# Preparing the next image in a fused two-layer kernel: vector steps three sample products apart, the norm's reciprocal in four pieces

## The chip, the cores and the metric

The kernel runs on one core of a Trainium2 chip. The metric is the device time of one execution in microseconds. Engines are named as in the profile: PE is TensorE's matmul and PEld its weight load, DVE is VectorE, ACT is ScalarE, POOL is GpSimd, SP is SyncE, which only issues DMAs here. A "q" after an engine's name is its sequencer.

## The reference

Two layers over x of shape (32, 128, 32, 32), each added to its input. Both begin with a group norm over 32 groups.

```python
# layer 0: a state-space block over the 1024 positions of an image
h = einsum('bdl,de->ble', u, W_enc) + b_enc        # 128 -> 1024
y = gelu(causal_conv(h, K of 64 taps) + D * h)
g = y @ W_glu + b_glu                              # 1024 -> 2048
g = g[..., :1024] * sigmoid(g[..., 1024:])
h = layernorm(h + g)
x = x + (h @ W_dec + b_dec)                        # 1024 -> 128

# layer 1: a deformable depthwise convolution, 8 x 8 taps
off = depthwise_conv_3x3(gn(x), offset_w) + offset_b   # 2 x 64 offsets a position
for each of 64 taps: acc += weight[c, tap] * bilinear(gn(x), position + tap + off)
x = x + gelu((acc - bn_mean) * bn_gamma / sqrt(bn_var + 1e-5) + bn_beta)
```

All of it is in float32.

## The kernel before

Three short stages build the convolution's kernel table, normalise the input and run layer 0's encoder and convolution; they end at about 2100 us and are not touched. The rest is `main_block`, which runs two generators side by side.

`first_part(b)` is the gate, norm and decoder of layer 0 for image b, in two halves of 512 positions. For each of eight groups m it runs eight matmuls for the gate (L707), eight for the value (L730) and one for the encoder (L746); the decoder (L639) follows one group late. ACT applies the sigmoid (L714), DVE multiplies (L738) and adds (L759), ACT squares (L767), and POOL sums (L641, L768). At the end of a half, `close` forms mean and variance with two matmuls and leaves the rest to five small closures. Each is put on a list by `later(n, work)`: after every matmul of the gate `tick()` counts down, and a closure runs when its count is out.

`second_part(b)` is layer 1 for image b as matmuls: 68 pieces, each with three sample products, which makes 204 steps. A piece needs two loads from DRAM, `ds` and `dhy` (hat functions of the sampling coordinates, 512 KB each at full width, L978 on SP's queue). DVE multiplies them (`weights`, L989) two pieces ahead of their use. Each step is one matmul (L1032) into one of four PSUM buffers, and a DVE multiply by the tap weights out of it (L1035); POOL adds up (L1044, L1049). There are five buffers for `ds` and four for `dhy`, and a load waits until its buffer is free. Pieces 32 to 35 have half the width, so steps 96 to 107 are short. Image windows `dxw` (L1003) are loaded on SP's queue as well.

`prepare(b + 1)` makes what `second_part(b + 1)` needs, in small closures put between the steps of `second_part(b)`. A list of pairs (step, closure) says before which of the 204 steps each is issued. In the order of the list before: `fetch` loads the image that layer 0 stored (L793, SP); `total`, `mean`, `variance` and `normal` are the group norm (ACT at L798, L805 and L813, tiny matmuls, DVE at L816 and L817); nine `taps` are the 3 x 3 offset convolution (DVE, L835 and L839); `largest` keeps the maximum (L847); `across` and `down` turn offsets into coordinates (L856, L867); `spread(0)` and `spread(1)` store them to DRAM with eight DMAs each (L874, SP); `turn(0)` and `turn(1)` transpose the image on PE (L922), copy it by ACT (L923) and store it (L926, ACT's queue); `gather(0)` and `gather(1)` load the coordinates spread out (L888, SP); 24 `hats` make the hat functions, two ACT instructions each (L903, L904) and a store of 312 KB (L905, ACT's queue); `ready` hands the image over.

Within an engine and within a queue, instructions keep the order in which the program issues them. `run_along` lets the generator that is behind in its own costs go next: a tick costs 863, a step its columns plus 40. An image takes 290 ticks and 204 steps. The tiles of the fetched image, the offsets, the coordinates, the transposed image and two tiles of the image's end share two buffers (tag `img`).

The last two images have no `first_part` beside them.

Of the kernel before, what the change touches and what calls it, by code (L numbers as in the profile page):

```python
# [14 lines left out]
P = 128  # L15
# [485 lines left out]
def main_block(nc, tc, const, ins, x, u_d, y_d, x1_d, out, offmax):  # L501
# [20 lines left out]
    with ctx:  # L522
# [78 lines left out]
        for i in range(2):  # L601
            t = dram1.tile([2, NCOL], F32, tag=f"rel_d{i}", name=f"rel_d{i}")
            flat = t.rearrange("a (p l) -> (a p) l", p=P // 2)
            n = 2 * NCOL // P
# [5 lines left out]
        def at(t, offset, ap):  # L610
            return bass.AP(tensor=t.tensor, offset=t.offset + offset, ap=ap)
# [22 lines left out]
        def temp(name):  # L634
            return tpool.tile([P, T], F32, tag="gt", name=name)
# [9 lines left out]
        def later(calls, work):  # L645

            soon.append([calls, work])
# [8 lines left out]
        def close(b, hf, sums, dec, xt):  # L656

            tag = f"{b}_{hf}"
            m1, d, rs = (temp(f"g{n}_{tag}") for n in ("m1", "d", "rs"))
            ps = pglu.tile([P, T], F32, tag="g", name=f"gpm_{tag}")  # L660
            nc.tensor.matmul(ps, const["davg"], sums[0], start=True, stop=True)
            nc.scalar.copy(m1, ps)
            ps = pglu.tile([P, T], F32, tag="g", name=f"gpq_{tag}")
            nc.tensor.matmul(ps, const["davg"], sums[1], start=True, stop=True)
            nc.scalar.activation(rs, m1, AF.Square)

            def variance():
                nc.vector.scalar_tensor_tensor(
                    d, m1, neg_g, dec, op0=ALU.mult, op1=ALU.add
                )  # L670
                nc.vector.tensor_sub(rs, ps, rs)

            def deviation():
                nc.scalar.activation(rs, rs, AF.Sqrt, bias=const["eps"])

            def scale():
                nc.vector.reciprocal(rs, rs)
                nc.vector.tensor_mul(d, d, rs)

            def add():  # L680
                nc.vector.scalar_tensor_tensor(xt, d, shift, xt, op0=ALU.add, op1=ALU.add)

            def store():
                nc.scalar.dma_start(x1_d[b, :, hf * T : hf * T + T], xt)
                stored.add((b, hf))

            later(2, variance)
            later(4, deviation)
            later(7, scale)
            later(8, add)  # L690
            later(11, store)

        stored = set()
        pending = {}
# [1 line left out]
        def first_part(b, last=False):  # L696
            for hf in range(2):
# [5 lines left out]
                for m in range(KD):  # L703
# [37 lines left out]
                    if "close" in pending:  # L741
                        close(*pending.pop("close"))
                        yield 2 * MM
                        tick()
# [26 lines left out]
            if last:  # L771
                decode(pending.pop("decode"))
                close(*pending.pop("close"))
                while soon:
                    yield MM
                    tick()
# [6 lines left out]
        def prepare(b):  # L783
# [37 lines left out]
            def taps(lo, hi):  # L821
                def run():
                    if lo == 0:
                        st["co"] = two.tile([P, L], F32, tag="img", name=f"dco_{b}")
                    co3 = st["co"].rearrange("p (h w) -> p h w", w=W)
                    v3 = st["v"].rearrange("p (h w) -> p h w", w=W)
                    for n in (4, 0, 1, 2, 3, 5, 6, 7, 8)[lo:hi]:
                        dy, dx = n // 3 - 1, n % 3 - 1
                        y0, y1 = max(0, -dy), H - max(0, dy)
                        x0, x1 = max(0, -dx), W - max(0, dx)  # L830
                        src = v3[:, y0 + dy : y1 + dy, x0 + dx : x1 + dx]
                        to = co3[:, y0:y1, x0:x1]
                        wn = off_w[:, n : n + 1]
                        if n == 4:
                            nc.vector.tensor_scalar(  # L835
                                to, src, wn, off_b, op0=ALU.mult, op1=ALU.add
                            )
                        else:
                            nc.vector.scalar_tensor_tensor(  # L839
                                to, src, wn, to, op0=ALU.mult, op1=ALU.add  # L840
                            )

                return run
# [25 lines left out]
            def spread(a):  # L869
                def run():  # L870
                    for ky in range(8):

                        g = a * 8 + ky
                        nc.sync.dma_start(  # L874
                            at(
                                rel_d[b % 2],
                                a * NCOL + ky // KY2 * NPIECE + 7 * SLOT + ky % KY2 * H,
                                [[7 * SLOT, 8], [8 * SLOT, W], [1, H]],
                            ),
                            st["rel"][g * 8 : (g + 1) * 8],  # L880
                        )

                return run

            def gather(a):
                def run():
                    t = st["t", a] = one.tile([P, HSUB], F32, tag=f"rel{a}", name=f"dr_{b}_{a}")
                    nc.sync.dma_start(  # L888
                        t, at(rel_d[b % 2], a * NCOL, [[HSUB, P], [1, HSUB]])
                    )  # L890

                return run

            def hat(a, k):


                def run():
                    if k == 0:
                        st[f"h{a}"] = dram.tile(
                            [(8, 16)[a], NCOL], F32, tag=f"hat_d{a}", name=f"dhat_{b}_{a}"  # L900
                        )
                    t = hatpool.tile([P, HSUB], F32, tag="hat", name=f"dh_{b}_{a}_{k}")
                    nc.scalar.activation(t, st["t", a], AF.Abs, bias=minus[:, k : k + 1])  # L903
                    nc.scalar.activation(t, t, AF.Relu, scale=-1.0, bias=const["one"])  # L904
                    nc.scalar.dma_start(  # L905
                        at(st[f"h{a}"], k * NCOL, [[HSUB, P], [1, HSUB]]), t
                    )

                return run

            hats = [hat(0, k) for k in range(8)] + [hat(1, k) for k in range(16)]

            def turn(n):


                def run():
                    if n == 0:
                        st["vt"] = two.tile([P, NCHUNK, C], F32, tag="img", name=f"dvt_{b}")
                    ps = psam.tile([P, 4, C], F32, tag="sam", name=f"dtr_{b}_{n}")
                    for i in range(4):  # L920
                        lo = (4 * n + i) * P
                        nc.tensor.transpose(ps[:, i, :], st["v"][:, lo : lo + P], ident)  # L922
                    nc.scalar.copy(st["vt"][:, 4 * n : 4 * n + 4, :], ps)  # L923
                    if n == 1:
                        st["vt_d"] = dram.tile([L, C], F32, tag="vt_d", name=f"dvt_d_{b}")
                        nc.scalar.dma_start(  # L926
                            st["vt_d"].rearrange("(n p) c -> p n c", p=P), st["vt"]
                        )

                return run  # L930

            def ready():
                images[b] = st["vt_d"], [st["h0"], st["h1"]]

            steps = [
                (34, fetch), (41, total), (43, mean), (46, variance), (48, normal),
                *((49 + i, taps(i, i + 1)) for i in range(9)),
                (58, largest), (59, across), (60, down), (61, spread(0)), (62, spread(1)),
                (64, turn(0)), (66, turn(1)),
                (68, gather(0)), (69, gather(1)),  # L940
                *((75 + 102 * i // len(hats), step) for i, step in enumerate(hats)),
                (178, ready),
            ]
            return steps
# [128 lines left out]
        def opening():  # L1073

            yield 30.0
            for _, step in prepare(0):
                step()
                yield 1.0
            for i in range(SB):
                load_hat(i, 0)  # L1080
            for i in range(HB):
                load_hat(i, 1)
            windows(0, 0)
            weights(0)
            weights(1)
# [5 lines left out]
        for b in range(B):  # L1091
            steps = prepare(b + 1) if b + 1 < B else []
            if b + 2 < B:
                run_along(
                    (first_part(b + 2, last=(b + 2 == B - 1)), FIRST),
                    (second_part(b, steps), SECOND),
                )
            else:
                run_along((second_part(b, steps), SECOND))
# [152 lines left out]
```

## Time and profile before

| | us |
|---|---|
| median of 9 runs | 14057.63 |
| range of the runs | 14050.15 to 14072.49 |
| the profiled execution | 14059.32 |
| its span, first to last instruction | 14057.3 |
| first sample step | 2329.6 |
| one image in the regular part | about 370 |
| image 30, without layer 0 beside it | 328 |

The profile is of one execution. Its page gives busy times and the chain of waits; further views give the waits by pair, the busy time in chosen windows and the instructions in order of time. A row of a timeline has start, length, engine, line, operation, result and operands, and in brackets the idle time before it and what ended it. Images are counted from 0; image 10 starts at 6023.0 us and image 11 at 6392.4. Step numbers of an image are found by counting the weight loads of L1032, two to a step.

### The profile page before, as it was taken

Reading aid. Unit: us, or ns where it says so; the run is one execution under the profiler, and the core shown is the slowest. Engines: PE = TensorE matmul, PEld = TensorE weight load, DVE = VectorE, ACT = ScalarE, POOL = GpSimd, SP = SyncE. Lnnn points to the kernel's source line nnn. Section 1 sums busy time; section 2 is a strip of 40 time slices with the busy share of each in tenths; the row PEclk is TensorE's granted clock in tenths of the full one; section 3 lists DMA queues with packets and bytes.
Section 4 is the critical chain, followed back from the end, with each engine's and each line's share of the span. In section 5 each row is a group of like instructions: output and inputs, shape, how many; then the busy total and the mean of one; then the engine's idle time right before and its main releaser. Section 6 shows DMA issues by size and latency. Waiting matters only on the chain.

```text
span 14057.3 us, 134776 instructions
## 1 busy us (share of the span) xinstructions
PE 13277.6 (94%) x40482; PEld 7323.1 (52%) x40482; DVE 8832.2 (63%) x12555; ACT 3216.8 (23%) x5422; POOL 9131.0 (65%) x9158
## 2 busy tenths in 40 slices
PE   5888889999999999999999999999999999999965
PEld 4777744555555555555555555555555555555533
DVE  6666614666666666666666666666666666666656
ACT  3445412222222222222122122222222222222210
POOL 1334313777777777777677777777777677777767
PEclk9999999999999999999999999999999999999977
DMA  6777724888888888888888888888888888888888
GB/s 224 232 233 229 222 79 125 238 237 233 233 232 230 233 234 236 239 234 232 229 232 228 230 230 230 229 234 237 238 236 232 231 231 231 234 236 235 231 227 233
DMA packets 1741840, 3172.55 MB, mean 226 GB/s; under 512 B 311218, under 2 KB 1030450, under 8 KB 1740082
## 3 DMA queue, kind: packets, MB, share of 16 engines
q1 hardware_dynamic: 1528498, 2708.63, 72.9%
q10 hardware_dynamic: 163456, 320.92, 6.4%
q0 software_dynamic: 49152, 134.28, 3.1%
q8 instruction: 329, 5.39, 0.2%
q14 instruction: 405, 3.32, 0.1%
HBM read 2697.07 MB, written 466.06 MB: 225 GB/s over the span
## 4 chain that ended last, share of the span: by engine, by line
PE 75%; DMA 10%; DVE 8%; POOL 3%; issue 2%; ACT 2%; SPq 1%; DVEq 0%; ACTq 0%; POOLq 0%
PE gpg L707 22%; PE gpv L730 21%; PE dps L1032 21%; DMA ds<-dhat 6%; PE psz L227 4%; PE gph L746 3%; PE gpo L639 3%; DVE dco L839 2%; DVE ds L989 2%; POOL y_d L296 2%; DMA y_d<-yo 1%; PE psy L266 1%; DMA dhy<-dhat 1%; DVE dp L1035 1%; ACT t L280 1%
## 5 line engine op out<-in xcount | busy, mean ns | idle before, releaser
L1032 PE MATMUL dps<-ds,dxw 128*128 128x256 f32 (+18 forms) x13056 | 4748.3, 451 | 293.9 <-DVE dp L1035 292.1
L1035 DVE TENSOR_TENSOR dp<-dps,k_weight_slots 128x256 f32<-128x256 f32 (+17 forms) x6528 | 3059.9, 484 | 2865.4 <-PE dps L1032 2566.1
L1049 POOL TENSOR_TENSOR dacc<-dacc,dp 128x256 f32<-128x256 f32 (+3 forms) x4736 | 4233.6, 894 | 371.5
L1044 POOL TENSOR_TENSOR dp<-dp 128x512 f32<-128x512 f32 (+3 forms) x2176 | 2865.2, 1317 | 2145.9 <-DVE dp L1035 2126.4
L1032 PEld LDWEIGHTS dps<-ds,dxw 128*128 128x128 f32 x13056 | 2482.8, 194 | 3323.5 <-issue 2521.1
L707 PE MATMUL gpg<-gy,g_w_glu 128*128 128x512 f32 x8192 | 3987.0, 593 | 22.8 <-DMA gy<-y_d 15.6
L730 PE MATMUL gpv<-gy,g_w_glu 128*128 128x512 f32 x8192 | 3974.4, 592 | 0.0
L989 DVE TENSOR_TENSOR ds<-ds,dhy 128x1024 f32<-128x1024 f32 (+3 forms) x2176 | 3162.2, 1453 | 1237.3 <-DMA ds<-dhat 1172.5
L707 PEld LDWEIGHTS gpg<-gy,g_w_glu 128*128 128x128 f32 x8192 | 1545.0, 190 | 1238.9 <-issue 976.1
L730 PEld LDWEIGHTS gpv<-gy,g_w_glu 128*128 128x128 f32 x8192 | 1548.7, 189 | 1158.1 <-issue 915.2
L767 ACT ACTIVATE gq<-gr 128x512 f32<-128x512 f32 x448 | 282.2, 630 | 5047.1 <-DVE gr L759 4719.8
L768 POOL TENSOR_TENSOR gs<-gs,gq 128x512 f32<-128x512 f32 x448 | 601.6, 1343 | 1262.8 <-ACT gq L767 1262.7
L266 PE MATMUL psy<-toe,z 128*128 128x192 f32 x4096 | 792.3, 354 | 223.8 <-DVE t L277 215.5
L266 PEld LDWEIGHTS psy<-toe,z 128*128 128x128 f32 x4096 | 737.9, 208 | 274.0 <-issue 212.4
L714 ACT ACTIVATE gs<-gpg,k_b_glu 128x512 f32<-128x512 f32 x512 | 351.9, 687 | 2154.6 <-PE gpg L707 2070.5
L903 ACT ACTIVATE dh<-dr,k_minus 128x624 f32<-128x624 f32 x768 | 620.6, 808 | 936.1 <-DMA dr<-rel_d 495.2
L296 POOL DMA_DIRECT2D y_d<-yo x1024 | 591.0, 584 | 353.0 <-ACT yo L290 325.6
L738 DVE SCALAR_TENSOR_TENSOR gs<-gpv,k_b_glu,gs 128x512 f32<-128x512 f32 x512 | 379.8, 742 | 413.3 <-PE gpv L730 413.3
L641 POOL TENSOR_TENSOR gs<-gs,gr 128x512 f32<-128x512 f32 x448 | 634.3, 1416 | 0.0
L904 ACT ACTIVATE dh<-dh,one 128x624 f32<-128x624 f32 x768 | 626.2, 815 | 24.9
L227 PE MATMUL psz<-w_enc,u 128*128 128x128 f32 x4096 | 581.7, 288 | 27.2 <-DVE z L234 11.7
L275 POOL MEMSET t<- 32x256 f32 x256 | 72.6, 323 | 775.7 <-ACT yo L290 774.9
(164 smaller groups left out, 6616.3 us busy)
## 6 DMA issues: line engine op xcount, KB each, us to landing
dhy<-dhat SPq DMA_DIRECT2D x1536, 512.0 KB
ds<-dhat SPq DMA_DIRECT2D x1536, 512.0 KB
dhat<-dh ACTq DMA_DIRECT2D x768, 312.0 KB
u<-u_d SPq DMA_DIRECT2D x256, 512.0 KB
y_d<-yo POOLq DMA_DIRECT2D x1024, 128.0 KB, 3.7
gy<-y_d SPq DMA_DIRECT2D x512, 256.0 KB
toe<-kp_d SPq DMA_DIRECT2D x128, 768.0 KB
dxw<-dvt_d SPq DMA_DIRECT2D x1248, 64.0 KB
```

Of the source, the lines that this page charges most:

```text
L227: nc.tensor.matmul(ps[:, j, :], u[:, (NB * g + j) * P : (NB * g + j + 1) * P], w_enc[:, k * P : (k + 1) * P], start=True, stop=True,)
L266: nc.tensor.matmul(ps[:, c // 2, c % 2, :], rows[i][:, g * CG + c0 + c, :], toe[:, c0 + c, :], start=True, stop=True,)
L296: nc.gpsimd.dma_start(y_d[d0 : d0 + CG, :, i * NB + j, :].rearrange("d b l -> b d l"), yo[i][j * B : (j + 1) * B],)
L641: nc.gpsimd.tensor_add(sums[0], sums[0], r)
L707: nc.tensor.matmul(gate, w_glu[:, k, D + m * P : D + m * P + P], ys[k], start=(k == 0), stop=(k == KD - 1),)
L730: nc.tensor.matmul(val, w_glu[:, k, m * P : m * P + P], ys[k], start=(k == 0), stop=(k == KD - 1),)
L904: nc.scalar.activation(t, t, AF.Relu, scale=-1.0, bias=const["one"])
L989: nc.vector.tensor_mul(s[:, :m], s[:, :m], hy[:, :m])
L1032: nc.tensor.matmul(ps, xw[:, j, :], s[:, :m, :, y0 : y0 + ny], start=True, stop=True)
L1035: nc.vector.tensor_mul(prod[:, :m, :, y0 : y0 + ny], ps, w[:, :, :, None].to_broadcast([P, m, KY2, ny]),)
L1044: nc.gpsimd.tensor_add(prod[:, :m, 0], prod[:, :m, 0], prod[:, :m, 1])
L1049: nc.gpsimd.tensor_add(to, to, prod[:, slot : slot + nj, 0])
```

## The change

In `close`, the reciprocal of the standard deviation is taken in four pieces of 128 columns, at ticks 7 to 10, where it was one instruction of 512 columns at tick 7; the multiply, the addition and the store follow four ticks later each. In `prepare`, the list of steps is rewritten: everything up to the norm comes six steps earlier, the nine taps stand three steps apart instead of one, the transposes come between them, the maximum, the coordinates, the spreads and the gathers come later and further apart, and the 24 hats start at step 96 instead of 75 and end at about the same step.

```diff
@@ -673,8 +673,10 @@
             def deviation():
                 nc.scalar.activation(rs, rs, AF.Sqrt, bias=const["eps"])
 
+            def invert(lo):
+                return lambda: nc.vector.reciprocal(rs[:, lo : lo + P], rs[:, lo : lo + P])
+
             def scale():
-                nc.vector.reciprocal(rs, rs)
                 nc.vector.tensor_mul(d, d, rs)
 
             def add():
@@ -686,9 +688,11 @@
 
             later(2, variance)
             later(4, deviation)
-            later(7, scale)
-            later(8, add)
-            later(11, store)
+            for n in range(4):
+                later(7 + n, invert(n * P))
+            later(11, scale)
+            later(12, add)
+            later(15, store)
 
         stored = set()
         pending = {}
@@ -933,12 +937,12 @@
                 images[b] = st["vt_d"], [st["h0"], st["h1"]]
 
             steps = [
-                (34, fetch), (41, total), (43, mean), (46, variance), (48, normal),
-                *((49 + i, taps(i, i + 1)) for i in range(9)),
-                (58, largest), (59, across), (60, down), (61, spread(0)), (62, spread(1)),
-                (64, turn(0)), (66, turn(1)),
-                (68, gather(0)), (69, gather(1)),
-                *((75 + 102 * i // len(hats), step) for i, step in enumerate(hats)),
+                (28, fetch), (35, total), (37, mean), (40, variance), (42, normal),
+                *((44 + 3 * i, taps(i, i + 1)) for i in range(9)),
+                (47, turn(0)), (50, turn(1)),
+                (71, largest), (74, across), (79, down), (81, spread(0)), (82, spread(1)),
+                (89, gather(0)), (90, gather(1)),
+                *((96 + 82 * i // len(hats), step) for i, step in enumerate(hats)),
                 (178, ready),
             ]
             return steps
```

## The prediction

> **What bounds the kernel now.** I read the page's busy shares first, then its chain of waits, then the waits summed over the regular stretch, then one image in windows, and last the timelines of three queues around the change.
>
> ```profile
> PE 13277.6 (94%) x40482; PEld 7323.1 (52%) x40482; DVE 8832.2 (63%) x12555; ACT 3216.8 (23%) x5422; POOL 9131.0 (65%) x9158
> PE 75%; DMA 10%; DVE 8%; POOL 3%; issue 2%; ACT 2%; SPq 1%; DVEq 0%; ACTq 0%; POOLq 0%
> ```
>
> TensorE sets the time; every other engine has a third or more free. So the change pays only where TensorE stands still. The waits from 2700 to 13430 us, which hold 29 images of some 370 us (total, times, longest):
>
> ```profile
> PEld dps L1032 <- DVE dp L1035: 242.8, 517, 2.4
> PEld gph L746 <- DVE gs L738: 40.6, 27, 3.2
> PEld gpg L707 <- DVE gs L738: 31.0, 29, 1.8
> DVE ds L989 <- DMA ds<-dhat: 937.1, 377, 8.9
> ```
>
> A weight load has about 0.24 us of idle before it even when nothing is late, so the first three rows hold 242.8 + 40.6 + 31.0 - 573 x 0.24 = 177 us of standstill behind VectorE, 6.1 us an image: the ceiling of what this change can win in the regular part. Its place I took from the timeline: for images 1 to 28, by how much two neighbouring weight loads are further apart than the median of such pairs, by sample step (204 an image, two L1032 loads each). VectorE is named for 1.67 us at steps 60 to 62, for 0.86 at 72 to 74 and 0.35 at 78 to 86, for 0.61 at 105 to 110 and for 1.36 at 117 to 119 (the gate at L738). The rest lies around step 12, before the change, and in scraps.
>
> One image in windows, cut at steps 48, 66, 75, 90, 96, 108, 120 and 144:
>
> ```profile
> 6107.40:6145.40 38.00, 36.37 (x101) 18.19 (x100) 37.73 (x41) 3.01 (x4) 28.24 (x19) 1.00 0.69 164
> 6145.40:6163.00 17.60, 17.29 (x48) 8.58 (x47) 6.49 (x10) 1.87 (x4) 10.77 (x10) 1.00 0.68 153
> 6163.00:6190.80 27.80, 27.80 (x76) 14.02 (x75) 16.54 (x24) 7.73 (x10) 18.33 (x19) 1.00 1.04 276
> 6190.80:6202.10 11.30, 11.30 (x32) 5.69 (x31) 7.33 (x12) 5.99 (x8) 8.78 (x9) 1.00 0.86 249
> 6202.10:6215.10 13.00, 13.00 (x48) 7.68 (x46) 8.09 (x15) 3.78 (x5) 8.87 (x10) 1.00 1.05 281
> 6215.10:6239.30 24.20, 22.78 (x61) 11.28 (x60) 13.27 (x21) 5.05 (x7) 12.46 (x13) 1.00 1.03 286
> 6239.30:6284.50 45.20, 45.20 (x122) 22.78 (x121) 32.09 (x42) 15.63 (x20) 31.35 (x27) 1.00 1.02 283
> ```
>
> After the stretch and its length stand PE, PEld, DVE, ACT and POOL busy, clock, DMA share, GB/s. In the first row, with the nine taps, the maximum and the two coordinate steps, VectorE is busy 37.73 of 38.00 us: there it is the bound. The DMA queues are half idle in the first two rows and then full, at 276 to 286 GB/s, until step 144. The end of that burst on VectorE, TensorE and SyncE:
>
> ```profile
> 6134.13 3.01 DVE L856 SCALAR_TENSOR_TENSOR drel<-dco,k_base_x 128x1024 f32<-128x1024 f32 x1
> 6159.53 1.23 DVE L989 TENSOR_TENSOR ds<-ds,dhy 128x1024 f32<-128x1024 f32 x1 [7.57 <-DMA ds<-dhat]
> ...
> 6137.68 0.98 PE L1032 MATMUL dps<-ds,dxw 128*128 128x416 f32 x2 [1.09 <-DVE dp L1035]
> ...
> 6141.56 12.85 SPq L874 DMA_DIRECT2D rel_d<-drel  x16
> ```
>
> TensorE waits for L1035 behind the 3.01 us of L856. SyncE then issues 16 coordinate stores for 12.85 us, the next piece's `ds` load stands behind them, and VectorE waits 7.57 us for it.
>
> [...]
>
> **The change part by part.** The sum stands on the profiled execution, 14059.32 us (span 14057.3).
>
> *The reciprocal in four.* L677 goes from one instruction of 512 columns to four of 128, one to a tick.
>
> ```profile
> L677 DVE RECIPROCAL grs<-grs 128x512 f32<-128x512 f32 x58 | 193.7, 3340 | 0.0
> L816 DVE RECIPROCAL gn_r<-gn_r 128x1 f32<-128x1 f32 x29 | 4.4, 153 | 0.0
> ```
>
> (3340 - 153) / 511 = 6.24 ns a column; a quarter is 0.15 + 0.79 = 0.95 us, four are 3.79. That adds 0.45 us to each of 64 half images, 29 us of VectorE. At steps 19 and 121 TensorE shows no standstill today (under 0.1 us), so it costs and saves nothing; the cover is VectorE's third of free time, and without it the price is 29 us. The multiply, the addition and the store come four ticks later. By the interleaving's costs (863 a tick, columns + 40 a step) the store moves from step 23, where the trace has it, to 25.
>
> *Fetch at 28.* From store to fetch 22.5 us become some 5. The fetch stands on SyncE's queue and waits until the store has landed, with the `dhy` and `ds` loads behind it. That landing isn't in the trace: 128 KB stores of `y_d` land in 3.7 us (page, part 6), 312 KB hat stores hold their buffer about 8. So SyncE waits 0 to 3 us; I take 2. `ds` loads there are issued about 12 us before their use without a wait, so nothing reaches TensorE; uncovered it would be 2 us an image. From fetch to the first ACT step there are 7 steps as before.
>
> *Taps every third step, maximum, coordinates at 71, 74, 79.* Same instructions, spread over 35 steps instead of 12. A piece of three steps lasts 5.6 us; VectorE has three products of 0.5, a weight product of 1.5 and 0.4 of the gate's work, 3.4 us; with a tap of 1.4 it is 4.8, still below. With L856 it is 6.4, 0.8 us over for one piece, and four product buffers carry more than that. The 1.67 us at 60 go: -1.67.
>
> *Transposes at 47 and 50.* Eight on TensorE, two ACT copies and the 512 KB store on ACT's queue, 17 steps earlier. ACT has nothing there (it sat 14 us before L767 at step 53). 0.
>
> *Spreads at 81 and 82, gathers at 89 and 90.* Still 16 issues. Their operand is ready 3 us before instead of late, and the transposed image's store no longer lies between them (SyncE stood some 3 us for it). About 10 us of issue. The loads behind them are for pieces 32 to 35, which have 512 columns instead of 1024, so half the bytes. `ds` for piece 32 is issued near step 86.5 and used at 90, 6.5 us: the wait of 7.5 us falls to 0 to 2. Of 0.86 + 0.35 I keep 0.2: -1.0. Bounds: all gone (-1.2), or all back at step 90 (0).
>
> *Hats from 96, every 3.4 steps instead of 4.25.* Between 89 and 120 come the two 312 KB gathers and some two more hats than before, less those of steps 75 to 92. The queues are full here, and what is late next is `ds` at 105 to 119. Upper bound: 1.28 MB at 286 GB/s = 4.5 us an image, all on TensorE. Lower bound: -2.0, if those stalls go because the lead is no longer lost at 66 to 75. The short steps begin with the buffers about as full as today (the queues caught up by 96: share 0.86). I take +0.6.
>
> Sum: -1.67 - 1.0 + 0.6 = -2.1 us an image, x 29 = -61. Image 30 has no gate work beside it, TensorE mostly waits for loads, and steps 54 to 72 took 5 us more than their neighbours: -5. Total -66: 13993; the median of the runs is 1.7 below the profiled one, so 13992.
>
> **The rivals.**
> - *The stall only moves.* The taps' 1.67 is won, the spread stalls as much at 90 as at 72, and the hats cost 1.6: nothing an image, 14052. For: the same 16 issues on the same queue. Against: half-size loads behind them.
> - *Slower: the DMA queues become the bound from 89 to 145.* Gathers and denser hats reach full queues, and their 4.5 us go whole to TensorE: -1.67 - 1.0 + 4.5 = +1.8 an image, x 29 = +53, less 5 at image 30: 14107. It decides once the extra standstill at 90 to 125 passes 2.7 us. For: shares of 1.03 to 1.05 there. Against: over the image the queues have slack (0.58 to 0.78 from step 144 on), and only a part of these bytes is new before 120.
> - *The whole ceiling.* With the lead kept, the stalls at 105 to 119 go too: -1.67 - 1.2 - 2.0 = -4.9 x 29 = -142, less 10 at image 30: 13907. For: the late `ds` from 72 on is one backlog. Against: steps 96 to 107 ask for four pieces in 13 us, whatever came before.
>
> **How the numbers follow.** Forecast 0.53, stall moves 0.17, slower 0.15, whole ceiling 0.15. A measurement of this kernel tells 0.2%, 28 us, from no change. The forecast's own range is 13960 to 14030; the unknown costs of the hats and the tail of the whole ceiling take it to 13930, the moved stall to 14060. Faster: nearly all of the forecast and the whole ceiling, 0.67; same 0.18; slower 0.15.
>
> **What would show it.** Right: no TensorE wait for L1035 at 44 to 74; VectorE under 90% there; DMA share from 48 to 80 without the dip; `ds` waits at 84 to 93 under 2 us; stalls at 105 to 119 near 2.5 us. Wrong: a `ds` wait of 5 us or more at 90, standstill over 4 us at 100 to 125, ACT waiting for hat stores long enough to make L714 late, or SyncE held by the fetch so long that `ds` is late at 30 to 45.

## The result and the profile after

The changed kernel takes 14006.62 us (median of 9 runs, 13990.78 to 14024.54). The kernel before, run again beside it, takes 14058.83 us (29 runs). The ratio is 0.9963, 95% interval 0.9955 to 0.9972: 52 us faster. The profiled execution has a span of 14002.5 us, 54.8 under that of before.

The page of the changed kernel: busy sums, and the chain of waits by engine.

```profile
PE 13253.5 (95%) x40482; PEld 7321.3 (52%) x40482; DVE 8804.1 (63%) x12747; ACT 3232.6 (23%) x5422; POOL 9160.7 (65%) x9158
PE 80%; DMA 9%; DVE 3%; ACT 3%; POOL 2%; issue 2%; SPq 1%; ACTq 0%; DVEq 0%; POOLq 0%
```

VectorE's share of the chain fell from 8% to 3%; its busy sum is no larger, although the reciprocals alone hold 25.5 us more, near the 29 they were priced at: 256 pieces of 939 ns are 239.3 us, 64 whole ones of 3341 ns were 213.8.

The waits of the changed kernel over the 29 regular images, 2700 to 13370 us (total, times, longest). All lines behind the edit are 4 higher: L1036 and L1039 are the sample matmul and product, L993 the weight product, L742 and L750 the gate.

```profile
DVE ds L993 <- DMA ds<-dhat: 644.5, 267, 8.3
ACT dh L907 <- DMA dhat<-dh: 545.4, 192, 7.9
PEld dps L1036 <- DVE dp L1039: 169.8, 408, 3.3
PEld gph L750 <- DVE gs L742: 37.8, 27, 2.6
PEld gpg L711 <- DVE gs L742: 25.6, 29, 1.6
```

The first three rows of the prediction's ceiling were 242.8 + 40.6 + 31.0 us, less 0.24 us for each of 573 waits: 177 us. Now they are 169.8 + 37.8 + 25.6 less 0.24 x 464: 122. So by this count a third of the ceiling was won. But the longest wait of L1036 rose from 2.4 to 3.3 us, which no removed stall explains.

Image 10 of the changed kernel in windows, cut at the same steps as before (48, 66, 75, 90, 96, 108, 120, 144; same columns):

```profile
6093.00:6128.10 35.10, 35.10 (x98) 17.81 (x97) 27.30 (x33) 2.53 (x4) 26.91 (x22) 1.00 0.87 211
6128.10:6145.40 17.30, 17.30 (x47) 8.68 (x46) 14.70 (x17) 0.69 (x1) 13.50 (x11) 1.00 0.76 191
6145.40:6173.20 27.80, 27.80 (x76) 14.03 (x75) 18.47 (x26) 1.95 (x3) 19.85 (x18) 1.00 0.67 165
6173.20:6184.50 11.30, 11.30 (x32) 5.69 (x31) 4.80 (x9) 3.84 (x5) 8.57 (x9) 1.00 0.81 222
6184.50:6197.50 13.00, 13.00 (x48) 7.68 (x47) 7.56 (x15) 3.78 (x5) 8.55 (x10) 1.00 1.04 271
6197.50:6221.40 23.90, 22.86 (x62) 11.31 (x61) 11.13 (x17) 6.69 (x9) 12.35 (x13) 1.00 0.83 242
6221.40:6270.80 49.40, 46.97 (x121) 23.26 (x120) 35.28 (x48) 17.81 (x23) 29.66 (x27) 0.97 1.03 284
```

Row one: 38.00 us became 35.10, and VectorE is busy 27.30 of them instead of 37.73. It is no longer the bound there. The DMA share of the first two rows rises from 0.69 and 0.68 to 0.87 and 0.76; the lowest row is now the third (0.67, before 1.04), where the spreads stand. Rows six and seven took 24.20 and 45.20 us before and take 23.90 and 49.40 now. Image 10 is the worst case: over images 1 to 28, steps 120 to 131 take 22.6 us in each image before, and 22.6 (in seven of them) to 26.9 (image 10) in the changed kernel. In row six the queues have gone from a share of 1.03 to 0.83: less full, not fuller, just ahead of the place where TensorE now stands.

The prediction counted weight loads that come later than usual. That count is larger than the time lost, since a load can be late while the matmul before it still runs. In the kernel before, image 10, 6151 to 6193 us, one load waits 1.1 us for VectorE, and TensorE itself only 0.3:

```profile
PEld dps L1032 <- DVE dp L1035: 1.4, 2, 1.1
PE dps L1032 <- DVE dp L1035: 0.3, 1, 0.3
```

In all the prediction's rows of image 10 TensorE is idle for 1.63 + 0.31 + 1.42 = 3.4 us, against the 6.1 us an image of the ceiling. So the table gives lengths: from the first load of a stretch of steps to the first load behind it, mean of images 1 to 28, in us. The first row is the kernel before, the others are differences from it.

| kernel | 12-23 | 30-59 | 60-62 | 63-71 | 72-92 | 105-119 | 120-131 | all steps |
|---|---|---|---|---|---|---|---|---|
| before | 19.17 | 57.69 | 6.87 | 18.72 | 40.58 | 27.92 | 22.56 | 370.03 |
| changed | -0.19 | +0.89 | -1.68 | -1.36 | -0.70 | -0.53 | +1.56 | -2.01 |
| 1: reciprocal only | -0.05 | 0.00 | 0.00 | 0.00 | +0.13 | +0.03 | 0.00 | +0.12 |
| 2: steps only | -0.07 | +0.95 | -1.68 | -1.36 | -0.70 | -0.16 | +6.38 | +3.36 |
| 3: taps only | -0.09 | +0.03 | -1.68 | -0.48 | +0.09 | +0.12 | 0.00 | -2.00 |
| 4: late steps only | -0.11 | +1.26 | -1.24 | -1.36 | -0.70 | -0.47 | +6.44 | +3.83 |
| 5: hat stores by GpSimd | -0.18 | +0.89 | -1.68 | -1.36 | -0.70 | +0.25 | 0.00 | -2.77 |
| 6: the same, reciprocal whole | -0.16 | +0.89 | -1.68 | -1.36 | -0.70 | +0.16 | +0.54 | -2.30 |
| 7: stores apart | -0.06 | +0.93 | -1.68 | -1.36 | -0.70 | -0.55 | +0.37 | -3.04 |
| 8: pause in the hats | -0.10 | +0.93 | -1.68 | -1.36 | -0.70 | -1.31 | +0.21 | -4.00 |
| 9: pause, four pieces | -0.01 | +0.89 | -1.68 | -1.36 | -0.70 | -1.17 | 0.00 | -4.03 |
| 10: longer pause | -0.07 | +0.89 | -1.68 | -1.36 | -0.70 | -1.25 | 0.00 | -4.16 |

The transposes' matmuls are part of these lengths: where they move from steps 64 and 66 to earlier ones, as in the changed kernel, some 0.9 us leaves 63 to 71 and appears at 30 to 59.

So the list removed what it was made to remove, and 1.6 us an image were lost anew at steps 120 to 131, where every image of the kernel before took the same 22.6.

What is late there is read from the timeline of the changed kernel, image 10, steps 111 to 122 (start, length, engine and line, operation; in brackets the idle time before it and what ended it).

```profile
6203.25 0.81 ACT L907 ACTIVATE dh<-dr,k_minus 128x624 f32<-128x624 f32 x1 [6.79 <-DMA dhat<-dh]
6204.54 0.55 SPq L982 DMA_DIRECT2D ds<-dhat  x1
6204.94 0.33 ACTq L909 DMA_DIRECT2D dhat<-dh  x1
...
6214.09 1.80 SPq L1007 DMA_DIRECT2D dxw<-dvt_d  x3
...
6216.63 0.57 SPq L982 DMA_DIRECT2D ds<-dhat  x1
...
6224.69 1.23 DVE L993 TENSOR_TENSOR ds<-ds,dhy 128x1024 f32<-128x1024 f32 x1 [8.29 <-DMA ds<-dhat]
...
6228.22 0.77 PE L1036 MATMUL dps<-ds,dxw 128*128 128x288 f32 x2 [2.43 <-DVE dp L1039]
```

SyncE issues nothing from 6205.1 to 6214.09. Then it issues three window loads, which have nothing to do with the hats of the next image, and only behind them the `ds` load whose data comes 8 us later; VectorE waits 8.29 us and TensorE 2.43. What held SyncE is in its own waits in the changed kernel, again over 2700 to 13370 us:

```profile
SPq L1007 <- DMA dhat<-dh: 270.3, 55, 9.0
SPq L982 <- DMA dhat<-dh: 223.2, 111, 8.0
```

In the kernel before there is one such row:

```profile
SPq L978 <- DMA dhat<-dh: 136.8, 81, 4.5
```

The semaphore events show the link. The 9,380 DMAs of SyncE and the 936 of ScalarE in this execution of the changed kernel stand in the trace in the order in which the program issues them, as do 12,744 instructions of VectorE, and each DMA names one of eight semaphores for its completion. Taken in the order of the two queues, these 10,316 DMAs fit one unbroken rotation of the eight. No DMA was issued before the one eight places ahead of it had landed: in all 10,308 pairs the last update of the semaphore that they share (the 16th of that DMA, for the coordinate stores the ninth) came before the issue, at the closest by 16 ns. The window load of 6214.09 stands eight places behind the hat store of 6204.94 and uses the same semaphore; that store landed at 6214.08. Likewise the `ds` load issued at 6203.29 stands eight behind the hat store of 6194.42, which landed at 6203.23.

So my reading after the result was: a hat every 3.4 steps puts a store that lands about 9 us after its issue (8.8 and 9.1 us for these two) eight places ahead of some of the loads. What makes `ds` late is then a wait on SyncE's queue, not a lack of bandwidth for the loads.

### The profile page after: what moved, and what is told of

Its sections match the earlier page's. It is cut to its first block, busy times and chain, and to the rows that moved or that the text cites. A ratio compares the mean times of both kernels' runs of the same rounds, so it can differ in the third digit from the quotient of the medians.

```text
span 14002.5 us, 135026 instructions
## 1 busy us (share of the span) xinstructions
PE 13253.5 (95%) x40482; PEld 7321.3 (52%) x40482; DVE 8804.1 (63%) x12747; ACT 3232.6 (23%) x5422; POOL 9160.7 (65%) x9158
## 4 chain that ended last, share of the span: by engine, by line
PE 80%; DMA 9%; DVE 3%; ACT 3%; POOL 2%; issue 2%; SPq 1%; ACTq 0%; DVEq 0%; POOLq 0%
PE gpg L711 23%; PE gpv L734 23%; PE dps L1036 22%; DMA ds<-dhat 5%; PE psz L227 3%; PE gph L750 3%; PE gpo L639 3%; DMA dhat<-dh 2%; POOL y_d L296 1%; PE psy L266 1%; DMA y_d<-yo 1%; ACT t L280 1%; DVE z L234 1%; ACT yo L286 1%; SPq L982 1%
## 5 line engine op out<-in xcount | busy, mean ns | idle before, releaser
L1039 DVE TENSOR_TENSOR dp<-dps,k_weight_slots 128x256 f32<-128x256 f32 (+17 forms) x6528 | 3078.0, 483 | 3051.1 <-PE dps L1036 2869.5
L1036 PE MATMUL dps<-ds,dxw 128*128 128x256 f32 (+18 forms) x13056 | 4737.4, 450 | 266.7 <-DVE dp L1039 264.6
L1053 POOL TENSOR_TENSOR dacc<-dacc,dp 128x256 f32<-128x256 f32 (+3 forms) x4736 | 4396.5, 928 | 371.4
L1036 PEld LDWEIGHTS dps<-ds,dxw 128*128 128x128 f32 x13056 | 2484.2, 193 | 3275.2 <-issue 2569.5
L1048 POOL TENSOR_TENSOR dp<-dp 128x512 f32<-128x512 f32 (+3 forms) x2176 | 2712.4, 1247 | 1985.5 <-DVE dp L1039 1982.9
L993 DVE TENSOR_TENSOR ds<-ds,dhy 128x1024 f32<-128x1024 f32 (+3 forms) x2176 | 3152.1, 1449 | 925.4 <-DMA ds<-dhat 860.1
L772 POOL TENSOR_TENSOR gs<-gs,gq 128x512 f32<-128x512 f32 x448 | 631.0, 1408 | 1337.1 <-ACT gq L771 1337.1
L742 DVE SCALAR_TENSOR_TENSOR gs<-gpv,k_b_glu,gs 128x512 f32<-128x512 f32 x512 | 380.0, 742 | 424.1 <-PE gpv L734 424.1
```

Of the source, the lines that this page charges most:

```text
L772: nc.gpsimd.tensor_add(sums[1], sums[1], sq)
L993: nc.vector.tensor_mul(s[:, :m], s[:, :m], hy[:, :m])
L1036: nc.tensor.matmul(ps, xw[:, j, :], s[:, :m, :, y0 : y0 + ny], start=True, stop=True)
L1039: nc.vector.tensor_mul(prod[:, :m, :, y0 : y0 + ny], ps, w[:, :, :, None].to_broadcast([P, m, KY2, ny]),)
L1048: nc.gpsimd.tensor_add(prod[:, :m, 0], prod[:, :m, 0], prod[:, :m, 1])
L1053: nc.gpsimd.tensor_add(to, to, prod[:, slot : slot + nj, 0])
```

## The experiments

Four runs split the change.

**1. The reciprocal in four pieces alone.** The kernel before with `invert` and the four ticks of the change, its list of steps as it was.

> The reciprocal in four pieces alone, the list of sample steps as before. My theory: it is off TensorE's path, so 14057 give or take 5 us (ratio 0.9995 to 1.0005), VectorE's busy sum up by 29 us or less, no new standstill of TensorE at steps 17 to 27. The rival (VectorE's short instructions do cost): up to 29 us more, ratio 1.002.

Measured: 14056.2 us against 14058.8, ratio 0.9998 (0.9990 to 1.0006). No cost and no gain, and no stretch is more than 0.13 us longer. VectorE's busy sum, 8739.3 us, is 93 under the 8832.2 of before in spite of the pieces, so their price is not seen in it.

**2. The new list alone.** The changed kernel with the reciprocal whole:

```diff
-            for n in range(4):
-                later(7 + n, invert(n * P))
-            later(11, scale)
-            later(12, add)
-            later(15, store)
+            later(7, scale)
+            later(8, add)
+            later(11, store)
```

> The new list of steps with the reciprocal whole. My theory: the whole gain of the change is the list's, so this run is the changed kernel within 5 us, about 14007 (ratio 0.9963); since the store is issued at step 23 instead of 25, SyncE waits for x_d less than the 3.2 us an image of the changed kernel. The rival: part of the gain comes from the four pieces, then this run is 10 to 29 us above the changed kernel.

Measured: 14157.6 us, ratio 1.0067 (1.0054 to 1.0081). Both expectations fall: the list alone is 99 us slower than before and 151 us slower than the changed kernel. The table puts it at steps 120 to 131, which are 6.38 us an image longer than before, in the changed kernel 1.56. Timeline of this run, image 10, steps 121 to 125:

```profile
6289.97 1.23 DVE L989 TENSOR_TENSOR ds<-ds,dhy 128x1024 f32<-128x1024 f32 x1 [8.06 <-DMA ds<-dhat]
...
6293.49 0.77 PE L1032 MATMUL dps<-ds,dxw 128*128 128x288 f32 x2 [2.19 <-DVE dp L1035]
6294.49 1.95 DVE L989 TENSOR_TENSOR ds<-ds,dhy 128x1024 f32<-128x1024 f32 x1
6297.82 3.35 DVE L677 RECIPROCAL grs<-grs 128x512 f32<-128x512 f32 x1 [1.39 <-ACT grs L674]
6301.21 0.69 DVE L678 TENSOR_TENSOR gd<-gd,grs 128x512 f32<-128x512 f32 x1
...
6302.29 0.86 PE L1032 MATMUL dps<-ds,dxw 128*128 128x352 f32 x2 [3.42 <-DVE dp L1035]
```

The late `ds` (8.06 us) leaves VectorE behind TensorE, and 8 us later comes the second half's reciprocal. VectorE first waits 1.39 us for its operand, then the reciprocal occupies it for 3.35 us in one piece, with the multiply behind. No product (L1035) is taken in these 5.4 us, and TensorE stands still a second time, for 3.42 us. In the changed kernel, after a wait of 1.38 us for the same operand, one product is taken between each piece of 0.95 us and the next. The part of the expectation on SyncE holds: there is no wait for `x_d` among its waits, which the changed kernel has for 90.1 us in 28 times (3.2 us an image).

**3. The early steps alone.** From the kernel before, with the rest of its list unchanged:

```diff
-                (34, fetch), (41, total), (43, mean), (46, variance), (48, normal),
-                *((49 + i, taps(i, i + 1)) for i in range(9)),
+                (26, fetch), (33, total), (35, mean), (38, variance), (40, normal),
+                *((41 + 2 * i, taps(i, i + 1)) for i in range(9)),
```

> From the kernel before, only the early steps move: fetch 26, taps at 41 + 2i (41 to 57), and the list from the maximum (58) on as before. My theory, after the trace of the change: the taps' stall of 1.67 us an image at steps 60 to 62 goes and nothing comes in its place, so -1.4 to -1.7 us an image, -40 to -50 us: about 14012 (ratio 0.9965 to 0.9972); the ds wait of 7.5 us behind the 16 stores stays, as does the standstill of 1.2 us at 72 to 86; no standstill of over 0.3 us at step 120. The rival (one backlog: the taps' stall and the later ones are the same lateness): the later ones shrink too, 13980 or less. The other rival (all of the gain comes from the late spread): 14050 or more.

Measured: 13981.59 us, ratio 0.9945 (0.9932 to 0.9959): 77 us faster than before and 25 under the whole change (0.9963). The mechanism is the expected one: steps 60 to 62 are 1.68 us shorter, the later places did not move (+0.09, +0.12, 0.00), and the `ds` wait at the piece of step 75 is 7.59 us where it was 7.53. So the backlog rival falls for all that lies behind step 72, although the time came out near its figure. The size is larger than expected, 2.00 us an image: another 0.48 went at steps 63 to 71, right behind the burst, for which the expectation had no term.

By image this run gains as much as the whole change (-2.00 and -2.01). In the profiled executions the 16 us between the two lie in the last two images (585 us here, 602 in the changed kernel).

**4. The late steps alone.** The kernel before with its burst of taps at 49 to 57 and the transposes at 58 and 61, and from the maximum on the list of the change; the reciprocal whole.

> From the kernel before, only the late steps move: taps stay nine in a row at 49 to 57, transposes at 58 and 61, then maximum 71, across 74, down 79, spreads 81 and 82, gathers 89 and 90, hats from 96 as in the change. My theory: the spread's standstill falls from 1.2 us to under 0.3, the taps' own is left at 0.3 to 1.7, and the denser hats bring the new standstill of about 1.4 + 0.8 us at steps 120 to 125, so 0 to +1 us an image: 14050 to 14085 (ratio 0.9995 to 1.002). The rival (the late spread brings the gain and the hats cost nothing): -1 us an image or more, 14025 or less.

Measured: 14165.9 us, ratio 1.0079 (1.0065 to 1.0093). The spread's loss goes (-0.70 at 72 to 92), but steps 120 to 131 are 6.44 us longer, as in run 2: here too the reciprocal is whole, and I had left it out of the expectation. The two runs agree: late hats with a whole reciprocal cost some 6.4 us an image behind step 120.

**5 and 6. The hat stores out of the turn.** The changed kernel, its hat stores issued by GpSimd one step after each hat. In the trace of the changed kernel GpSimd's 1,024 DMAs name eight other semaphores, none of which a DMA of SyncE or ScalarE names; the bytes stay.

```diff
-                    nc.scalar.dma_start(
-                        at(st[f"h{a}"], k * NCOL, [[HSUB, P], [1, HSUB]]), t
-                    )
+                    st["hat", a, k] = t
...
+            def keep(a, k):
+                def run():
+                    nc.gpsimd.dma_start(
+                        at(st[f"h{a}"], k * NCOL, [[HSUB, P], [1, HSUB]]), st["hat", a, k]
+                    )
+                return run
...
-                *((96 + 82 * i // len(hats), step) for i, step in enumerate(hats)),
+                *((96 + j + 82 * i // len(hats), step)
+                  for i in range(24) for j, step in ((0, hats[i]), (1, keeps[i]))),
```

> The changed kernel, its 24 hat stores an image issued by GpSimd one step after the hat instead of by ScalarE: same bytes, same steps, but no longer among the DMAs of SyncE and ScalarE that take their completion semaphores in turn. My theory (SyncE's loads stand behind hat stores through that turn): SyncE's waits for hat stores at steps 108 to 116, 12.6 us an image, fall under 2; the 6.5 us wait of VectorE for ds at step 123 under 2.5; the standstill of 2.4 us at 120 to 128 under 0.6, so about -1.8 us an image, -50 us: 13950 to 13970, if GpSimd's own waits cost nothing. The rival (the bytes of the denser hats fill the queues): the ds wait at 123 stays at 5 to 7 us and the time within 10 us of 14007 or above.

Measured: 13983.79 us, ratio 0.9947 (0.9933 to 0.9960), 23 us under the changed kernel. SyncE's waits name no hat store any more. Waits of this run over 2700 to 13370 us:

```profile
ACT dh L907 <- DMA dhat<-dh: 932.8, 349, 7.4
DVE ds L1001 <- DMA ds<-dhat: 420.7, 200, 6.1
PEld dps L1044 <- DVE dp L1047: 82.4, 293, 2.0
```

The hat buffers come free later than in the changed kernel (932.8 us of waiting in place of 545.4), and still VectorE waits for `ds` only 420.7 us instead of 644.5. At the piece of step 123 its wait is 2.04 us instead of 6.54, and steps 120 to 131 are as short as before, not 1.56 us longer. The queues are fuller meanwhile, as the row of steps 108 to 120 of image 10 shows (DMA share 1.03 against 0.83 in the changed kernel):

```profile
6228.10:6252.99 24.89, 23.15 (x61) 11.13 (x60) 12.78 (x20) 7.68 (x11) 14.80 (x18) 1.00 1.03 271
```

With the same bytes, fuller queues and `ds` on time, that decides between the two theories. The time misses its expectation by 14 us for two reasons: the first image's hats, which nothing covers, make the start of the image loop 31 us later (2362.2 against 2331.0), and steps 105 to 119 are 0.78 us longer than in the changed kernel, where TensorE now waits for a copy of ScalarE's (L662) in more than half of the images and longer for the gate. ScalarE waits more for hat buffers in this run, which fits, but I did not test it.

> As the run before, with the reciprocal whole again. The list alone, with the reciprocal whole, took 14158; the theory of its 151 us is that one 3.3 us instruction at step 124 comes just after the late ds, when the product buffers are used up. Then with ds on time the whole reciprocal costs nothing: within 15 us of the run before. The rival (the four pieces are needed by the new list for another reason, such as the store's place): again 100 us or more above it.

Measured: 13999.75 us, ratio 0.9956 (0.9942 to 0.9969). The whole reciprocal costs 16 us here, against 151 with `ds` late: +0.54 us at 120 to 131 in place of 0.00. The ranges of the two runs overlap, so the 16 us are rough; they lie just outside the 15 that were expected. So its price depends on how far VectorE is ahead of TensorE when it comes, its lead.

**7. Eight stores at a time.** The taps of run 3, transposes earlier, the 16 coordinate stores in two groups (kernel before as base):

```diff
+                (44, turn(0)), (46, turn(1)),
+                (58, largest), (60, across), (61, down), (62, spread(0)), (69, spread(1)),
+                (72, gather(0)), (80, gather(1)),
+                *((77 + 101 * i // len(hats), step) for i, step in enumerate(hats)),
```

> The early taps of the taps-only run (13982), with the transposes at 44 and 46 and the 16 coordinate stores in two groups of eight, at 62 and 69, the gathers at 72 and 80, hats evenly from 77. My theory (what counts is how long SyncE is held at once, against a lead of 15 to 20 us there): the ds wait of 7.6 us at step 75 goes, and the standstill at 72 to 86 falls from 2.2 us to about 0.6, -1.6 us an image, -45 us: 13925 to 13950. The rival (the queues, full from 72 on with gathers and hats, make ds late there, not the burst of issues): 13970 or more, ds waits of 4 us or more at 75 to 92 still there.

Measured: 13960.42 us, ratio 0.9928 (0.9915 to 0.9942). What became of the stores is seen in two timelines, steps 63 to 76 of image 10. Run 3:

```profile
6125.87 13.29 SPq L874 DMA_DIRECT2D rel_d<-drel  x16
...
6139.26 0.52 SPq L978 DMA_DIRECT2D ds<-dhat  x1
...
6144.22 1.23 DVE L989 TENSOR_TENSOR ds<-ds,dhy 128x1024 f32<-128x1024 f32 x1 [7.40 <-DMA ds<-dhat]
```

Run 7:

```profile
6121.47 4.62 SPq L874 DMA_DIRECT2D rel_d<-drel  x8
...
6126.18 0.52 SPq L978 DMA_DIRECT2D ds<-dhat  x1
...
6131.40 9.66 SPq L874 DMA_DIRECT2D rel_d<-drel  x8
...
6141.78 0.54 SPq L978 DMA_DIRECT2D ds<-dhat  x1
...
6145.14 1.48 DVE L989 TENSOR_TENSOR ds<-ds,dhy 128x1024 f32<-128x1024 f32 x1
```

Sixteen stores in one go hold the loads for 13.3 us, and VectorE waits 7.40. In two groups the `ds` loads between them keep the lead, although the second group alone takes 9.66 us, and the weight product starts with no wait for DMA, with nothing moved to a place of smaller loads. Steps 72 to 92 are 0.70 us shorter than before, in run 3 0.09 longer. This run also has the transposes earlier and the gathers later and apart; how much of the effect the split alone has is argued from the timelines, not tested. The time is 10 us above its expectation: steps 120 to 131 are 0.37 us longer, where the whole reciprocal again meets a `ds` that was late (2.15 us).

**8. A pause in the hats.** As run 7, but

```diff
-                *((77 + 101 * i // len(hats), step) for i, step in enumerate(hats)),
+                *((77 + 2 * i, step) for i, step in enumerate(hats[:8])),
+                *((110 + 68 * i // 16, step) for i, step in enumerate(hats[8:])),
```

> As the run before, but the first 8 hats every 2 steps from 77 to 91, none from 92 to 109, and the other 16 evenly from 110 to 173. If the standstill at 105 to 119 (2.5 us an image) comes from hats in the queues while steps 96 to 107 ask for four pieces in 13 us, 1 us of it or more goes: 30 us or more under the run before, about 13900. The rival (the four pieces in 13 us are enough by themselves, or the dense hats from 77 on make ds late at 84 to 95): the same as the run before or slower.

Measured: 13929.76 us, ratio 0.9910 (0.9897 to 0.9924): 31 us under run 7 and 124 under the kernel before. Steps 105 to 119, which run 5 had not shortened, are 0.76 us shorter than in run 7, and VectorE's wait for `ds` at 114 to 119 falls from 4.3 to 3.1 us an image. SyncE waits for no hat store at 105 to 119 in run 7, so the turn of the semaphores isn't what the pause relieves there. That the queues count at this place fits, but ScalarE also has fewer hats to make in the pause, and the two were not separated. The waits of this run over 2700 to 13310 us:

```profile
DVE ds L990 <- DMA ds<-dhat: 370.3, 224, 4.7
PEld dps L1033 <- DVE dp L1036: 126.5, 463, 2.0
PEld gph L746 <- DVE gs L738: 18.7, 22, 1.7
```

VectorE's wait for `ds`, 937.1 us in the kernel before, is down to 370.3; TensorE's for the gate to less than half.

**9 and 10. The pause with four pieces, and a longer pause.** Run 8 with `invert`, everything up to the second spread one or two steps later; and with the last 16 hats at 115 to 174.

> The pause of the run before (13930) with the reciprocal in four pieces, and everything up to the second spread one or two steps later, so that the fetch (28) still comes after the store. My theory: the standstill of 0.54 us at step 123 behind the whole reciprocal goes, -0.4 to -0.5 us an image, about -15 us: 13910 to 13920. The rival (the pieces cost elsewhere what they give, as beside the old list, where they changed nothing): 13925 or more.

> As the run before, with the pause up to step 114: the 16 hats of the second half from 115 to 174, every 3.9 steps instead of 4.25. If the rest of the gate's standstill at step 117 (0.62 us) comes from the hats at 110 and 114, it falls to 0.3 or less, about -10 us against the run before. If the denser hats after it hold SyncE as they did in the changed kernel (every 3.4 steps), a ds wait of over 3 us appears at 120 to 140 and the time is 10 us or more above.

Measured: 13928.21 us (ratio 0.9911, 0.9898 to 0.9925) and 13934.08 us (0.9913, 0.9900 to 0.9927). Both expectations miss. In run 9 what was left at step 123 goes as foreseen, but in length it was 0.21 us an image and not the 0.54 of the late loads from which I had expected 15 us; and steps 105 to 119 give back 0.14. In run 10 the gate at step 117 still holds TensorE (-1.25 at 105 to 119 against -1.17), and no `ds` wait for a piece of steps 120 to 140 passes 3 us. Hats every 3.9 steps do not bring the changed kernel's loss; what else differs between the two, the start at 115 after a pause, is not separated. Runs 8 to 10 are one time.

## Why the prediction was right, and where it was not

The direction and the size were right (13992 foreseen, 66 us less; 14006.62 measured, 52 less). But its terms were off by up to half a microsecond each and happened to cancel, and the largest risk was covered by an edit that I had priced at nothing; in that it was luck.

- **The ceiling, 6.1 us an image.** It counts late loads, of which TensorE covers a part; its rows of image 10 have 3.4 us of idle TensorE. The terms at steps 72 to 119 were sized by that count.
- **Taps, -1.67 us an image.** Shown: -1.68 at 60 to 62 in the changed kernel, and by itself in run 3. Run 3 has another -0.48 right behind, at 63 to 71.
- **Spreads and gathers, -1.0 of 1.2.** The waits went as foreseen: no `ds` wait from step 24 to 105, against my 0 to 2 us. In length it was -0.70. The reason given, half-size loads behind the stores, is not needed for it: run 7 reaches the same with the stores in two groups among full-size loads.
- **Taps, priced at 1.4 us each.** Their length goes with GpSimd. Over the 29 regular images of the kernel before, the 145 taps of L839 that begin while GpSimd is idle take 1.20 to 1.24 us, the 87 that begin while a GpSimd instruction runs 1.38 to 1.93, median 1.68. In the changed kernel it is 1.21 to 1.24 us for 58 and 1.27 to 1.88, median 1.38, for 174.
- **Fetch, 2 us of SyncE's waiting without effect.** It is 3.2, and nothing reaches TensorE.
- **Transposes, 0.** What they cost moved with them (-0.88 at 63 to 71, +0.86 at 30 to 59, from run 3 to the changed kernel).
- **Hats, +0.6 at 105 to 119.** This step failed. Steps 105 to 119 became 0.53 us shorter, and 120 to 131 became 1.56 longer: together +1.0. I had looked for the price in full queues ("what is late next is `ds` at 105 to 119"). What the runs show is SyncE held behind hat stores by the turn of eight semaphores, at a DMA share of 0.83 in the window ahead. The rival that made the queues the bound had the right place for a loss, and the wrong mechanism and size. By the prediction's count the late loads at 100 to 125 come to about 4 us (3.9 to 4.5, by which pairs of loads are compared), so one of its own signs of being wrong was there or nearly so.
- **Reciprocal, 0 on the path.** Right beside the old list (run 1), wrong beside the new one. I asked whether 0.45 us more work would find cover; the question was how long VectorE is closed to products, 3.35 us in one piece and the waits around it, and what lead it has at step 124. Without the split the change would have been 99 us slower than before (run 2). I added the edits as if each stood alone.
- **Image 30, -5.** It is -14.1 (327.9 to 313.8). Run 3, with the taps alone, has -5.6, as priced. The rest comes with the later spreads and hats: steps 60 to 92 of this image took 62.3 us before, 61.3 in run 3 and 44.1 in the changed kernel, which gives part of that back behind them.
- **Image 31, not priced.** It has no preparation beside it and is 17.4 us longer in this profiled execution (270.6 to 288.0); over all profiles it lies between 262.5 and 288.0 without pattern. It may be spread between executions. But the medians of run 3 and of the changed kernel differ by 25 us with equal regular images in their profiles, so a lasting part isn't excluded; its cause stays open.

The account of the span: 30 images with layer 0 beside them x -1.96 = -59, image 30 -14, image 31 +17, start +1: -55, against -54.8. Of a regular image's -2.0 the table has -1.68 and -0.48 from the taps, -0.70 from the later spreads, -0.53 at 105 to 119, -0.19 at 12 to 23, which I had not priced, and +1.56 at 120 to 131.

The rivals: "the stall only moves" was true in part: of some 3.6 us an image that went, 1.6 came back, but at 120 to 131 and not at 90. "The whole ceiling" did not come in this kernel; runs 8 to 10 reach 117 to 124 of the 150 us that it promised. (The sums of "slower" and "whole ceiling" leave out the 1.7 us between the profiled execution and the median, which changes nothing.)

## What to carry to other kernels

A step that is moved off one stall is to be checked for what its DMAs stand in front of, in the order in which DMAs are issued over all queues that share completion semaphores (here SyncE's and ScalarE's), not only for bytes: here a store that landed 9.1 us after its issue held an unrelated load. A long instruction on an engine that feeds the critical one costs according to the lead at that moment: the same reciprocal cost 4.8 us an image between run 2 and the changed kernel, and 0.5 between runs 6 and 5. So two edits can each look neutral and together decide the sign; test them apart and together. A lateness count is not a length: size the terms of a sum by the length of a stretch, from boundary to boundary. Two readings of these runs, not tested by themselves: put work that issues many DMAs in groups shorter than the lead of the loads behind them, and leave it out where the main loop asks for its loads fastest.

## What the runs showed of the hardware that I had not expected

- In the 10,308 pairs of the changed kernel, a DMA of SyncE or ScalarE was issued only after the one eight places earlier in the common order of both had landed, whatever they moved. Waits of SyncE for hat stores alone took 493.5 us over 29 images (270.3 + 223.2), up to 9.0 us at once; with the hat stores on GpSimd there was none. Run 5, with the same bytes and at steps 108 to 120 of image 10 a DMA share of 1.03 in place of 0.83, shows that the queues' bandwidth did not set it.
- Two 312 KB stores landed 8.8 and 9.1 us after their issue, at DMA shares of 1.03 and 0.85, though ScalarE spent 0.33 us on issuing one.
- Hat stores issued by GpSimd one step after the hat left ScalarE waiting longer for buffers (932.8 us in place of 545.4), and the image loop started 31 us later (2362.2 against 2331.0).
- The reciprocal's quarter took 939 ns, the mean of 256, where 0.95 us had been worked out from the lengths of one column and of 512.
